# Two parts a row with borders that return every 16 steps, in all four sweeps of a recurrent convolution

## The chip, the cores and the metric

The kernel runs on one core of a Trainium2 chip. A core has five engines that run side by side: TensorE (PE, with its weight loads PEld) multiplies matrices, VectorE (DVE) and ScalarE (ACT) work element by element, GpSimd (POOL) does too and more slowly, and SyncE (SP) issues transfers. Each takes its instructions from a queue of its own and waits at semaphores for the others. Matmul results land in PSUM[...]; everything else lies in SBUF[...]. The metric is the device time of one execution in microseconds, lower is better.

## The reference

Four layers work on an image of 48 channels and 128 x 128 pixels in fp32, each added to its input: an attention over all pixels, sweeps, a patch convolution with an FFT, and a state-space scan. The change is in the second layer. `step` there is a recurrence: the next row is the input row plus a convolution of the row just computed, with five taps along the row and 48 x 48 channels.

```python
def step(w, b):
    def f(carry, inp):
        nxt = inp + _conv1d(carry, w, b)
        return (nxt, nxt)
    return f
xs = jnp.moveaxis(x, 2, 0)
d0 = xs[0]
_, d_rest = jax.lax.scan(step(down_w, down_b), d0, xs[1:])
D = jnp.concatenate([d0[None], d_rest], 0)
seq = jnp.concatenate([D[Hh - 3::-1], D[Hh - 1:Hh]], 0)
u0 = D[Hh - 1]
_, u_rest = jax.lax.scan(step(down_w, down_b), u0, seq)
...
_, r_rest = jax.lax.scan(step(right_w, right_b), r0, ws[1:])
...
_, l_rest = jax.lax.scan(step(left_w, left_b), l0, R[Ww - 2::-1])
```

So there are four sweeps of 127 steps each: down and up over rows, right and left over columns, and each step needs the whole of the step before it.

## The kernel before

`attention`, `sweeps`, `patch_conv` and `scan` are called one after the other. `sweeps` gets two large SBUF tiles: `other` (xb in the profile), whose view `t` holds the image by rows with three padding rows and columns, and `xq` (xa), whose view `u` holds it by columns. Partitions 0 to 47 and 64 to 111 hold the same channels one pixel apart, so that one matmul covers two taps, and three matmuls (`i` in 0, 1, 2) cover the five taps and the bias. ScalarE normalises the input into `t` in chunks of rows (34 instructions at line 699), while the down sweep already runs behind it. In the up sweep ScalarE copies finished rows into `u` (`turn`, line 735). After the up sweep's rows are free, SP loads x1 back into `other` (line 784), and in the left sweep GpSimd adds the finished columns to it (line 788), and VectorE takes statistics of the sum (`stretch`, line 750).

The recurrence is a chain: matmuls of a step, VectorE's addition (line 769), matmuls of the next step. To keep TensorE busy while VectorE adds, a row of 129 places is cut into parts, and the parts are issued in turn: `advance(n, m, lo, hi)` (line 755) issues for part m of step n six matmuls into `sums_of[m][n % 2]`, each a PSUM bank, and one addition. An fp32 matmul shows in the profile as two matmul records with a weight load each, so a part has twelve. A place needs two neighbours to either side of the step before, so the border between two parts moves two places to the left with every step: a part then needs nothing of the part to its right. `parts` (line 728) writes these borders: `cuts` start to the right of their middle place, end to the left of it, and jump back after `length` steps. At the jump the left part has to wait for the right part of the step before.

`plan` (line 771) uses three parts and 12 steps for down, up and right, and two parts and 16 steps for left. `act`, `pe` and `dve` are wrapped in `InOrder`, which keeps each engine's instructions of this stage in the order in which they are written. Instructions of other stages may be put between them by the scheduler. One such is of interest: `packed_weights` of `patch_conv` loads two weight tables on ScalarE's queue (lines 109 and 111) and multiplies them on VectorE (line 112), and line 825 adds a bias. Their places in VectorE's queue lie within the down sweep.

```python
cuts = [L * m // streams + size - 1 - 2 * at for m in range(1, streams)]
yield first + k, list(zip([0, *cuts], [*cuts, L]))
```

Of the kernel before, what the change touches and what calls it, by code (L numbers as in the profile page):

```python
# [19 lines left out]
F32 = mybir.dt.float32  # L20
# [9 lines left out]
CH = 512  # L30
# [620 lines left out]
def sweeps(ctx, tc, xq, other, x1, const, ins):  # L651
# [10 lines left out]
    ps = ctx.enter_context(tc.tile_pool(name="l1_ps", bufs=1, space=PSUM))  # L662
# [27 lines left out]
    keep_running(nc.tensor, idle, const["ident"], some, 2)  # L690
    off = pool.tile([C, 1], F32, name="off")
    nc.vector.scalar_tensor_tensor(off, mean, -1.0, rstd, ALU.mult, ALU.mult)
    sums_of = [[ps.tile([128, CH], F32, name=f"p{m}{k}") for k in range(2)] for m in range(3)]
    for p in sums_of[0] + sums_of[1] + sums_of[2]:
        nc.vector.memset(p[0:K, 0:L], 0.0)
    act = InOrder(tc, nc.scalar)
    for lo, hi in [(0, 2), (2, 8)] + [(r, r + 8) for r in range(8, H, 8)]:
# [19 lines left out]
    steps = []  # L717
# [8 lines left out]
    down, up, right = H - 1, 2 * (H - 1), 3 * (H - 1)  # L726

    def parts(first, count, streams, length):

        for k in range(count):  # L730
            at, size = k % length, min(length, count - k // length * length)
            cuts = [L * m // streams + size - 1 - 2 * at for m in range(1, streams)]
            yield first + k, list(zip([0, *cuts], [*cuts, L]))

    def turn(h):

        for at, y in ((0, E + h), (64, E + h - 1)):
            act.copy(
                u[at : at + C, :, y : y + 2].rearrange("c w y -> c y w"),
                t[0:C, E + h : E + h + 2, E : E + W],  # L740
            )
# [8 lines left out]
    def stretch():  # L750
        _, xr = todo.pop(0)
        dve.bn_stats(const["st2"][:, len(done), :], xr)
        done.append(xr)

    def advance(n, m, lo, hi):

        which, out, inp, state = steps[n]
        p = sums_of[m][n % 2]
        for i in range(3):
            for at, a, b in ((0, max(lo, 1), hi), (64, lo, min(hi, L - 1))):  # L760
                pe.matmul(
                    p[at : at + C, a:b],
                    lhsT=w[0:K, which, i, at : at + C],
                    rhs=state[0:K, 2 * i + a : 2 * i + b],
                    start=(i == 0),
                    stop=(i == 2),
                )
        here = slice(E - 1 + lo, E - 1 + hi)
        dve.tensor_add(out[0:K, here], p[0:K, lo:hi], inp[0:K, here])

    plan = [
        *parts(0, up, 3, 12),
        *parts(up, right - up, 3, 12),
        *parts(right, len(steps) - right, 2, 16),
    ]
    for n, streams in plan:
        for m, (lo, hi) in enumerate(streams):
            advance(n, m, lo, hi)
        if down <= n < up and (n - down) % 2 == 0:
            turn(H - 2 - (n - down))  # L780
        if n + 1 == up:

            for r in range(0, N, 2048):
                nc.sync.dma_start(other[0:C, r : r + 2048], x1[:, r : r + 2048])
        x = 4 * (H - 1) - 1 - n
        if n >= right and x in sums:
            xr = sums[x]
            nc.gpsimd.tensor_add(  # L788
                xr,
                xr,  # L790
                u[0:C, x : x + xr.shape[2], E : E + H].rearrange("c w h -> c h w"),
            )
            step = CH // 2 // xr.shape[2]
            todo += [(n + 8, xr[:, r : r + step]) for r in range(0, H, step)]
        if todo and n >= todo[0][0]:
            stretch()
# [823 lines left out]
def tile_kernel(ctx: ExitStack, tc: tile.TileContext, ins: dict, out: bass.AP):  # L1620
# [10 lines left out]
    with ExitStack() as image:  # L1631
        xp = image.enter_context(tc.tile_pool(name="image", bufs=1))


        const["l1_w"] = xp.tile([128, 3, 3, 64 + C], F32, name="l1_w")
        xa = xp.tile([128, W * (W + 6)], F32, name="xa")
        xb = xp.tile([128, (H + 6) * (W + 6)], F32, name="xb")
        for i in range(0, N // 2, 2048):
            nc.gpsimd.memset(xb[32:64, i : i + 2048], 0.0)
            for half in range(2):  # L1640
                at = half * N // 2 + i
                nc.sync.dma_start(
                    xb[64 * half : 64 * half + C, i : i + 2048], ins["x"][:, at : at + 2048]
                )
        nc.sync.dma_start(const["l1_w"], ins["l1_w"])
        attention(tc, xa, xb, x1, const, ins)
        sweeps(tc, xa, xb, x1, const, ins)
        patch_conv(tc, xb, xa, x3, const, ins)
        scan_stats(tc, const)
# [198 lines left out]
```

## Time and profile before

| what | us |
|---|---|
| runs | 7446.85, 7449.31, 7458.15; median 7449.31 |
| the profiled execution, its own time | 7442.33 |
| its span, first to last instruction | 7440.4 |
| attention, about | 0 to 3785 |
| sweeps: first to last addition | 3786.99 to 4309.82 |
| patch convolution and start of the scan | from 4310 |
| first scan instruction of VectorE | 4780.5 |
| last scan instruction of VectorE starts | 7417.4 |

The profile is of one execution. Engine names are as above; a group or timeline line gives start and length in us, the engine, the source line, the operation, the tiles written and read, the shape, how many instructions are merged, and in brackets the idle time of the engine before it and what released it. L48 is the line of the `InOrder` helper, so all wrapped instructions carry it, and tiles tell them apart: `p<-xb,l_w` is a matmul of the down or up sweep, `p<-xa,l_w` one of the right or left sweep. Starts and lengths are of this execution only, and ends of matmuls are modelled. The costliest groups of the sweeps on the page are these:

| group of the page | count | busy us | mean ns |
|---|---|---|---|
| matmul p<-xb,l_w (down, up) | 9144 | 227.6 | 213 |
| matmul p<-xa,l_w (right, left) | 7620 | 229.3 | 218 |
| addition xb<-p,xb | 762 | 154.0 | 203 |

Matmuls overlap, so the mean length of one is not the distance between two.

### The profile page before, as it was taken

Reading aid. Unit: us, or ns where it says so; the run is one execution under the profiler, and the core shown is the slowest. Engines: PE = TensorE matmul, PEld = TensorE weight load, DVE = VectorE, ACT = ScalarE, POOL = GpSimd, SP = SyncE. Lnnn points to the kernel's source line nnn. Section 1 sums busy time; section 2 is a strip of 40 time slices with the busy share of each in tenths; the row PEclk is TensorE's granted clock in tenths of the full one; section 3 lists DMA queues with packets and bytes.
Section 4 is the critical chain, followed back from the end, with each engine's and each line's share of the span. In section 5 each row is a group of like instructions: output and inputs, shape, how many; then the busy total and the mean of one; then the engine's idle time right before and its main releaser. Section 6 shows DMA issues by size and latency. Waiting matters only on the chain.

```text
span 7440.4 us, 230057 instructions
## 1 busy us (share of the span) xinstructions
PE 6069.1 (82%) x106542; PEld 3125.0 (42%) x106542; DVE 3510.9 (47%) x3414; ACT 4386.6 (59%) x4744; POOL 2803.7 (38%) x603
## 2 busy tenths in 40 slices
PE   8999999999999999999988999555545645554565
PEld 3333333333333333333367865244434434344444
DVE  7300000000000000000045544599999999999998
ACT  2566666666666666666634013466666666666665
POOL 1000000000000000000010122499999999999998
PEclk9999999999999999999999999776766767766666
DMA  3000000000000000000000010365566666656675
GB/s 66 8 4 4 4 3 4 4 3 4 4 3 4 4 3 4 4 4 3 4 12 21 4 48 19 89 166 153 165 159 165 158 159 158 162 157 165 180 181 146
DMA packets 182477, 486.35 MB, mean 65 GB/s; under 512 B 35972, under 2 KB 67763, under 8 KB 179603
## 3 DMA queue, kind: packets, MB, share of 16 engines
q1 hardware_dynamic: 174679, 464.21, 24.3%
q8 instruction: 835, 13.68, 0.8%
q10 hardware_dynamic: 6827, 7.35, 0.4%
q14 instruction: 136, 1.11, 0.1%
HBM read 427.91 MB, written 22.02 MB: 60 GB/s over the span
## 4 chain that ended last, share of the span: by engine, by line
PE 62%; DVE 23%; issue 7%; POOL 4%; ACT 2%; DMA 1%; SPq 0%; ACTq 0%; DVEq 0%; POOLq 0%
PE acc L48 24%; PE s L48 24%; DVE h L1595 21%; PE p L48 7%; POOL h L1588 3%; PE y L48 3%; PE pv L48 1%; PE pp L48 1%; PE pc L48 1%; PE po L48 1%; ACT dA L48 1%; DMA du<-rep 1%; DVE y L48 0%; POOL y L991 0%; POOL y L992 0%
## 5 line engine op out<-in xcount | busy, mean ns | idle before, releaser
L48 ACT ACTIVATE e<-s,absT 128x1024 f32<-128x1024 f32 x2048 | 2276.8, 1114 | 1197.6 <-PE s L48 1196.7
L1588 POOL TENSOR_TENSOR h<-du,bt 128x3072 f32<-128x3072 f32 (+1 forms) x386 | 2559.5, 6668 | 86.3 <-DMA du<-rep 61.0
L48 PE MATMUL s<-xa,xb 49*64 49x512 f32 x16384 | 2124.2, 588 | 1.3 <-POOL xb L320 1.3
L48 PE MATMUL acc<-e,xb 64*64 64x512 f32 x16384 | 2124.2, 588 | 1.0 <-ACT e L48 1.0
L1595 DVE TENSOR_TENSOR_SCAN h<-dA,carry,h 128x1024 f32<-128x1024 f32 x864 | 1939.9, 2324 | 42.6 <-ACT dA L48 27.4
L48 ACT ACTIVATE dA<-dt,a 128x1024 f32<-128x1024 f32 x1152 | 1287.3, 1118 | 871.2 <-DVE h L1595 860.2
L48 PE MATMUL y<-h,cw 128*32 128x48 f32 x49152 | 905.0, 247 | 926.9 <-issue 495.6
L421 DVE TENSOR_TENSOR both<-o 128x512 f32<-128x512 f32 x31 | 21.5, 692 | 2958.5 <-ACT o L48 2854.8
L681 POOL MEMSET xb<- 32x2064 f32 x8 | 14.6, 1819 | 3500.4 <-PE acc L48 3491.3
L48 PEld LDWEIGHTS y<-h,cw 128*32 128x32 f32 x49152 | 815.0, 141 | 1054.2 <-issue 650.9
L48 PEld LDWEIGHTS s<-xa,xb 49*64 49x64 f32 x16384 | 629.7, 132 | 1132.4 <-issue 581.8
L48 PEld LDWEIGHTS acc<-e,xb 64*64 64x64 f32 x16384 | 629.3, 132 | 1133.1 <-issue 1109.9
L1595 DVE TENSOR_TENSOR_SCAN h<-dA,h 128x1024 f32<-128x1024 f32 x288 | 635.6, 2270 | 42.9 <-ACT dA L48 35.0
L48 PE MATMUL yz<-ev,sel 128*8 128x48 f32 x4096 | 193.2, 260 | 275.5 <-ACT ev L48 264.3
L48 PEld LDWEIGHTS yz<-ev,sel 128*8 128x8 f32 x4096 | 162.5, 106 | 332.2 <-ACT ev L48 297.0
L48 PE MATMUL p<-xb,l_w 112*48 112x43 f32 (+20 forms) x9144 | 227.6, 213 | 41.6 <-issue 32.0
L48 PE MATMUL p<-xa,l_w 112*48 112x43 f32 (+30 forms) x7620 | 229.3, 218 | 25.9 <-issue 18.2
L48 PEld LDWEIGHTS p<-xb,l_w 112*48 112x48 f32 x9144 | 216.8, 125 | 53.2 <-issue 42.0
L48 PEld LDWEIGHTS p<-xa,l_w 112*48 112x48 f32 x7620 | 207.0, 125 | 48.1 <-DVE xa L48 23.0
L48 DVE TENSOR_TENSOR xb<-p,xb 112x54 f32<-112x54 f32 (+3 forms) x762 | 154.0, 203 | 111.9 <-PE p L48 65.6
L788 POOL TENSOR_TENSOR xb<-xb,xa 48x2048 f32<-48x2048 f32 (+2 forms) x10 | 45.0, 4502 | 422.0 <-DVE xa L48 398.8
L48 PE MATMUL pc<-wt,xa 128*128 128x288 f32 x768 | 198.1, 415 | 0.0
(204 smaller groups left out, 3148.2 us busy)
## 6 DMA issues: line engine op xcount, KB each, us to landing
du<-rep SPq DMA_DIRECT2D x768, 256.0 KB
dt<-rep SPq DMA_DIRECT2D x768, 256.0 KB
rep<-dd SPq DMA_DIRECT2D x24, 192.0 KB
yd<-ys ACTq DMA_DIRECT2D x256, 12.0 KB
rest<-xa SPq DMA_DIRECT2D x90, 38.0 KB
xb<-in_x_dram SPq DMA_DIRECT2D x8, 384.0 KB
xres<-in_x_dram SPq DMA_DIRECT2D x32, 96.0 KB
x<-xa SPq DMA_DIRECT2D x32, 96.0 KB
```

What stands on the lines that cost most here:

```text
L48: ins = method(*args, **kwargs).ins
L421: nc.vector.tensor_add(self.both, o[:, 0], o[:, 1])
L681: nc.gpsimd.memset(b[32:64, some, inside], 1.0)
L788: nc.gpsimd.tensor_add(xr, xr, u[0:C, x : x + xr.shape[2], E : E + H].rearrange("c w h -> c h w"),)
L1588: nc.gpsimd.tensor_mul(h[:, p, ks], du.unsqueeze(1).to_broadcast([128, ks.stop - ks.start, LC]), r["bt"][:, ks],)
L1595: nc.vector.tensor_tensor_scan(h[:, p, k, :], dA, h[:, p, k, :], carry[:, i, k : k + 1] if ci else 0.0, ALU.mult, ALU.add,)
```

## The change

The first three sweeps get the cut of the fourth: two parts, borders that return every 16 steps. As `parts` now runs over two sweeps at a time (down and up, right and left, 254 steps each), the groups of 16 continue across the turn. The third pair of PSUM banks and its two memsets go.

```diff
-    sums_of = [[ps.tile([128, CH], F32, name=f"p{m}{k}") for k in range(2)] for m in range(3)]
-    for p in sums_of[0] + sums_of[1] + sums_of[2]:
+    sums_of = [[ps.tile([128, CH], F32, name=f"p{m}{k}") for k in range(2)] for m in range(2)]
+    for p in sums_of[0] + sums_of[1]:
         nc.vector.memset(p[0:K, 0:L], 0.0)
...
-    plan = [
-        *parts(0, up, 3, 12),
-        *parts(up, right - up, 3, 12),
-        *parts(right, len(steps) - right, 2, 16),
-    ]
-    for n, streams in plan:
+    for n, streams in [*parts(0, up, 2, 16), *parts(up, len(steps) - up, 2, 16)]:
         for m, (lo, hi) in enumerate(streams):
             advance(n, m, lo, hi)
```

In the built programs the instructions of attention, patch convolution and scan stand in the same order before and after. In the sweeps, VectorE's queue has 131 additions ahead of the weights' product (line 112) before the change and 93 after it; lines below the edit carry numbers smaller by five after it (825 becomes 820).

## The prediction

> **What bounds the kernel now.** I read the page's chain of waits first, then the table of windows for the four sweeps, then the timelines of TensorE and VectorE inside them. The chain says that the end of the program is reached through TensorE for most of the span:
>
> ```profile
> PE 62%; DVE 23%; issue 7%; POOL 4%; ACT 2%; DMA 1%; SPq 0%; ACTq 0%; DVEq 0%; POOLq 0%
> ```
>
> Attention, sweeps, patch convolution and scan follow each other, so time saved inside the sweeps stays saved unless their first or last wait changes. The windows, one line a sweep (down, up, right, left; columns: busy time of PE, PEld, DVE, ACT, POOL with counts, granted clock, DMA share, GB/s):
>
> ```profile
> 3786.00:3920.00 134.00, 114.61 (x4582) 109.70 (x4582) 78.29 (x382) 39.64 (x33) 16.31 (x18) 0.99 0.06 16
> 3920.00:4055.00 135.00, 113.02 (x4572) 107.10 (x4567) 77.31 (x382) 83.27 (x127) 0.00 (x0) 1.00 0.11 25
> 4057.00:4190.00 133.00, 114.42 (x4557) 109.17 (x4553) 77.27 (x380) 0.00 (x0) 0.00 (x0) 0.98 0.03 7
> 4190.00:4310.00 120.00, 113.94 (x3048) 96.86 (x3048) 71.76 (x312) 0.00 (x0) 58.19 (x27) 1.00 0.01 3
> ```
>
> Each sweep has 127 steps of 129 columns. The left one, already in two parts, is 13 to 15 us shorter than the others although VectorE also does statistics in it and GpSimd additions. It has 3048 matmul records (127 x 2 parts x 6 x 2 passes) against 4572. The same line of code thus runs in both forms in this one trace. TensorE's timeline says why, first a piece of the right sweep, then of the left:
>
> ```profile
> 4103.13 3.08 PE L48 MATMUL p<-xa,l_w 112*48 112x42 f32 x128 [0.67 <-issue]
> 4107.15 3.37 PE L48 MATMUL p<-xa,l_w 112*48 112x49 f32 x128 [0.94 <-issue]
> 4110.90 3.08 PE L48 MATMUL p<-xa,l_w 112*48 112x52 f32 x128 [0.38 <-issue]
> ...
> 4205.31 14.73 PE L48 MATMUL p<-xa,l_w 112*48 112x78 f32 x384 [0.35 <-DVE xa L48]
> ```
>
> With three parts TensorE stops for 0.4 to 0.9 us after every 128 matmuls, and nothing that the profile shows released it ("issue"). With two parts 384 run without a stop, and only the restart of the borders (16 steps) makes a wait for VectorE. 128 matmuls with their 128 weight loads are 256 instructions, and the instruction queue q8 moves 13.68 MB in 835 packets, 16.4 KB each: one packet is one such run.
>
> [...] here a block lasts 3.08 us and the next begins 3.75 us after the one before (4107.15 to 4110.90). [...] after the pause before 3834.31 the window 3834.10:3837.50 has clock 0.51. [...]
>
> **The change part by part.**
>
> *1. The step.* Three sweeps lose a third of their matmuls, weight loads and additions: 381 steps x 1 part, so 381 x 12 = 4572 matmul records and 381 additions of about 0.2 us. The columns stay 129. The price of a two-part step is read from the restarts (the 79-column additions) of the left sweep on VectorE's timeline:
>
> ```profile
> 4205.97 0.48 DVE L48 TENSOR_TENSOR xa<-p,xa 112x79 f32<-112x79 f32 x2 [0.72 <-PE p L48]
> ...
> 4221.05 0.48 DVE L48 TENSOR_TENSOR xa<-p,xa 112x79 f32<-112x79 f32 x2 [0.72 <-PE p L48]
> ```
>
> 15.08 us for 16 steps, restart included: 0.9425 us a step, 39 ns a matmul, so a block of 128 lasts 5.03 us and the 3.75 us refill fits, with 1.28 us to spare. Now the present spans. Down and up, from first to last addition: 3786.99 to 4054.61, 267.6 us. Right and left: 4057.00 to 4309.82, 252.8 us. After, each pair is one run of 254 steps: 254 x 0.9425 = 239.4, less some 0.4 because the last group is short and ends without the wait for its successor: 239.0. Gain 28.6 + 13.8 = 42.4 us.
>
> *2. What the gain must give back.* VectorE's queue holds, between the sweeps' additions, the product of the next stage's weights (L112). In the built program it stands behind 131 additions before (43 2/3 steps) and behind 93 after (46 1/2 steps): later in steps, earlier in time. Its inputs do not move: their DMAs are issued by ScalarE, behind its 34 normalisations, whose waits name none of the sweep's additions.
>
> ```profile
> 3785.01 41.27 ACT L48 ACTIVATE xb<-xa,off,gn_rstd 48x256 f32<-48x256 f32 x34 [0.47 <-DVE off L692]
> ...
> 3826.31 0.36 ACTq L109 DMA_DIRECT2D w<-in_l_w_dram  x1
> ...
> 3834.01 1.36 DVE L112 TENSOR_TENSOR wt<-wt,w 128x1152 f32<-128x1152 f32 x1 [2.22 <-DMA beta<-in_l_beta_dram]
> ...
> 3834.31 1.94 PE L48 MATMUL p<-xb,l_w 112*48 112x46 f32 x39 [2.58 <-issue]
> ```
>
> So the data is there at 3834.0 in both. After, the 93rd addition ends near 3787.0 + 43.3 = 3830.3 (two groups of 15.08 and fourteen faster steps of about 0.91, plus its own 0.24). VectorE then waits 3.7 us, multiplies for 1.36, and two additions later does L825 for 0.45; behind it stand the next addition and therefore TensorE. 5.5 us, less about 0.3 for the addition that is ready meanwhile: 5.2. (The before spans contain their own such hole, so nothing is subtracted twice.) TensorE is idle for over 3 us, so one window of 3.4 us at half clock follows: there 96 matmuls of 43 columns took 3.4 us (4062.80:4066.20, clock 0.51), 35 ns each; for 64 columns I estimate 53 ns against 39, 0.9 to 1.0 us lost. I take 1.0 (bounds 0 and 2).
>
> *3. The turn from up to right.* VectorE's pause of 2.39 us before 4057.00 lies between my two spans and remains: it is two copies of ScalarE of 0.65 us and what follows. The half-clock window behind it remains too, 1.0. The fetch stall of 1.92 us before 4062.21, beside the last reload of x1 (0.79 MB), is inside the present span; with 1.28 us to spare I leave 0.5 of it (0 to 1.9).
>
> *4. The rest.* At the start, step 1 still waits for its row (0.68 us before 3788.36): 0.3. The two memsets of PSUM that go are free, TensorE's warm-up matmuls end later than they do. ScalarE's turning copies, 128 x 0.658 = 84 us, still fit under an up sweep of 120 us. GpSimd's additions in the left sweep keep their place in steps; the eight reloads that they read are issued on SP during the up sweep, the last at 4055.97, and the first addition comes at 4204.4, still over 130 us later. No other instruction of any queue is moved, and the work behind the sweeps is the same.
>
> Given back: 5.2 + 1.0 + 1.0 + 0.5 + 0.3 = 8.0. **Net 34.4 us.** The profiled execution took 7442.33 (span 7440.4), so 7407.9 on its own terms. It lay 7.0 below the median of the runs, 7449.31; the difference is what carries over, so the forecast is 7449.3 - 34.4 = **7415 us**.
>
> **The rivals.**
> *A, the holes cost nothing:* the whole 42.4, 7407. For it: the left rate includes work on VectorE that the others lack. Against: the wait at the weights follows from two times that don't move. 12 in 100.
> *B, the fetch binds again:* eight reloads of 384 KB run in the up sweep beside the refills. If each cost the 1.92 us seen at 4062.21, 15.4 us go and 7430 is left. Against: in the present up sweep, with no slack at all, the loss against the down sweep is about 1 us in all (135 against 134 us). 8 in 100.
> *C, slower: the clock.* The new sweeps issue a third fewer matmuls[...]. At 53 ns a matmul a step takes 24 x 53 = 1.27 us, 0.33 more; from 34.4 / 0.33 = 104 of the 381 steps on it decides against the change, and over all of them it gives 7415 + 126 = 7541. Against: the left sweep had clock 1.00 over 120 us with TensorE 95% busy. 5 in 100.
> That the change does not do what it says is excluded: the built program has 79 to 49 columns a part from the first step on.
>
> **How the numbers follow.** The forecast has 75 in 100. Its own range: the step rate to 0.01 us over 381 steps is 4 us, the holes 3, and the runs before differ by 11 among themselves, so a median may be off by 5; together 7404 to 7428, which also takes in A and part of B, and leaves C and the rest of B out. A measurement of this kernel can tell about 0.2%, 15 us, from no change. Faster by more: 75 + 12 + 5 of B = 92; within: 3 of B; slower: C, 5.
>
> **What would show it.** Right: runs of TensorE of 384 matmuls from the down sweep on, no "issue" stops of 0.4 to 0.9 us there; additions of 79 columns every 15.1 us; each of the four sweeps near 120 us, the down one near 126; a pause of VectorE before L112 of 3 to 4 us with its end at an unmoved 48 us after the first normalisation. Wrong: clock near 0.5 in the first three windows, "issue" stops in the up sweep, or L112 released later than that.

## The result, and the profile after

| | kernel before | changed kernel |
|---|---|---|
| runs | 7441.78 to 7458.15, median 7448.68 (5 runs) | 7408.55 to 7415.31, median 7409.21 (5 runs) |
| profiled execution, its own time | 7442.33 | 7415.31 |
| span of that execution | 7440.4 | 7413.5 |

The ratio after to before is 0.9949, with a 95% interval of 0.9934 to 0.9963: 28 to 49 us faster, the medians 39.5 apart. The forecast was 7415, 34.4 us below 7449.3, the median of the three runs known then; the measured median lies inside its range of 7404 to 7428.

The profiled pair is only 26.9 us apart, so the stages have to be told apart before anything is explained. The additions of the sweeps, of the changed kernel, are these (count, then duration minimum/median/maximum in ns, then the start of the first and of the last one, then shapes):

```profile
L48 DVE TENSOR_TENSOR xb<-p,xb x508: 200/226/243, 3786.3 to 4031.1; 112x77 f32<-112x77 f32 x6, 112x54 f32<-112x54 f32 x6, 112x71 f32<-112x71 f32 x6, 112x60 f32<-112x60 f32 x6
L48 DVE TENSOR_TENSOR xa<-p,xa x508: 184/225/242, 4033.6 to 4273.0; 112x77 f32<-112x77 f32 x6, 112x54 f32<-112x54 f32 x6, 112x71 f32<-112x71 f32 x6, 112x60 f32<-112x60 f32 x6
```

With the last addition's own length the four sweeps run from 3786.25 to 4273.27. The same starts and ends, with the first scan instruction of VectorE and the span, cut each execution into four stages:

| profiled execution | first addition at | sweeps | to the first scan instruction | scan to the end |
|---|---|---|---|---|
| before | 3787.0 | 522.8 | 470.7 | 2659.9 |
| changed | 3786.3 | 487.0 | 469.1 | 2671.2 |
| changed, run again (e10, below) | 3786.1 | 487.7 | 471.0 | 2667.1 |

The sweeps are 35.8 us shorter, and 487 comes out twice. The 11 us that the profiled execution of the changed kernel lost are in the scan, whose instructions are the same and whose length differs by 10 us and more between executions (among all profiles of this study from 2652 to 2671; why, no run shows). That is why a pair of executions says little, and medians or the stage itself must be compared. The windows of the changed kernel, one line a sweep, with the columns of the prediction's table (the column before the last two is the granted clock):

```profile
3786.00:3911.00 125.00, 114.47 (x3052) 98.44 (x3047) 58.87 (x257) 38.79 (x32) 16.30 (x18) 0.97 0.05 16
3911.00:4031.50 120.50, 112.57 (x3036) 95.58 (x3036) 57.39 (x254) 83.15 (x127) 0.00 (x0) 1.00 0.12 26
4033.00:4154.00 121.00, 114.18 (x3068) 97.60 (x3066) 57.38 (x255) 0.00 (x0) 0.00 (x0) 0.99 0.03 7
4154.00:4273.50 119.50, 113.13 (x3036) 95.99 (x3030) 71.88 (x310) 0.00 (x0) 58.24 (x27) 1.00 0.01 3
```

All four now look like the old left sweep, with about 3050 matmul records instead of 4570 and the clock near 1; down alone is some 5 us longer. TensorE's timeline inside the right sweep, where it had stopped after every 128 records (a timeline line joins records of several shapes and names the first; inside it no gap is longer than 0.15 us):

```profile
4094.32 14.72 PE L48 MATMUL p<-xa,l_w 112*48 112x78 f32 x384 [0.35 <-DVE xa L48]
...
4109.38 14.73 PE L48 MATMUL p<-xa,l_w 112*48 112x78 f32 x384 [0.35 <-DVE xa L48]
```

384 records run without an "issue" stop, one border cycle of 15.06 us from line to line, as read from the old left sweep. Over all four sweeps, TensorE's "issue" stops (us in total, times, longest) were before:

```profile
PE p L48 <- issue: 50.2, 80, 2.6
```

and are after the change:

```profile
PE p L48 <- issue: 0.8, 2, 0.5
```

The instruction queue q8 has 799 packets in the whole kernel where it had 835: 36 fewer, and the 4572 records that went are 35.7 blocks of 128. And VectorE where the weights' product stands in its queue:

```profile
3829.25 0.48 DVE L48 TENSOR_TENSOR xb<-p,xb 112x76 f32<-112x76 f32 x2 [0.45 <-PE p L48]
3831.36 1.36 DVE L112 TENSOR_TENSOR wt<-wt,w 128x1152 f32<-128x1152 f32 x1 [1.63 <-DMA wt<-in_l_dw_dram]
3832.64 0.35 DVE L48 TENSOR_TENSOR xb<-p,xb 112x78 f32<-112x78 f32 x2
3832.90 0.45 DVE L820 TENSOR_TENSOR wt<-wt,bdw 128x288 f32<-128x288 f32 x1
3833.60 0.24 DVE L48 TENSOR_TENSOR xb<-p,xb 112x80 f32<-112x80 f32 x1 [0.25 <-PE p L48]
3835.06 0.24 DVE L48 TENSOR_TENSOR xb<-p,xb 112x79 f32<-112x79 f32 x1 [1.21 <-PE p L48]
```

The wait that was foretold is there, shorter (1.63 us). VectorE took its queue in order here, as the prediction assumed: the next addition, of 78 columns, starts at 3832.64, behind the product, though TensorE had ended its matmuls at 3830.4. After it the additions come more slowly for a while. The clock column of four windows explains this:

```profile
3830.00:3834.00 4.00, 1.05 (x32) 0.78 (x26) 2.23 (x5) 0.00 (x0) 0.00 (x0) 0.93 0.33 99
3834.00:3838.00 4.00, 4.00 (x72) 3.99 (x72) 1.14 (x5) 0.00 (x0) 0.00 (x0) 0.50 0.02 4
3838.00:3842.00 4.00, 3.98 (x95) 3.73 (x93) 1.57 (x7) 0.00 (x0) 0.00 (x0) 0.72 0.00 0
3842.00:3846.00 4.00, 3.91 (x114) 3.39 (x112) 2.03 (x9) 0.00 (x0) 0.00 (x0) 1.00 0.02 6
```

TensorE had 2.5 us with nothing to do, and then ran at half clock (0.50) for 6.8 us, from 3833.4 to 3840.2: 72 matmul records in 4 us instead of the 110 of such a window at clock 1.00 (3834 to 3838 in e3, below).

### The profile page after: what moved, and what is told of

Same layout as the page of the kernel before. It is cut to its first block, busy times and chain, and to the rows that moved or that the text cites. A ratio compares the mean times of both kernels' runs of the same rounds, so it can differ in the third digit from the quotient of the medians.

```text
span 7413.5 us, 220408 instructions
## 1 busy us (share of the span) xinstructions
PE 6051.7 (82%) x101970; PEld 3057.1 (41%) x101970; DVE 3451.0 (47%) x3031; ACT 4389.3 (59%) x4744; POOL 2804.1 (38%) x603
## 4 chain that ended last, share of the span: by engine, by line
PE 61%; DVE 22%; issue 7%; POOL 5%; ACT 2%; DMA 2%; SPq 0%; ACTq 0%; DVEq 0%; POOLq 0%
PE acc L48 24%; PE s L48 24%; DVE h L1590 20%; PE p L48 7%; POOL h L1583 4%; PE y L48 3%; DMA du<-rep 1%; PE pv L48 1%; PE pp L48 1%; PE pc L48 1%; PE po L48 1%; DVE xb L48 1%; ACT dA L48 1%; ACT xb L48 1%; DVE y L48 0%
## 5 line engine op out<-in xcount | busy, mean ns | idle before, releaser
L48 PE MATMUL p<-xb,l_w 112*48 112x78 f32 (+8 forms) x6096 | 227.5, 224 | 19.3 <-DVE xb L48 8.9
L48 PE MATMUL p<-xa,l_w 112*48 112x78 f32 (+8 forms) x6096 | 227.5, 224 | 14.4 <-DVE xa L48 5.5
L48 PEld LDWEIGHTS p<-xb,l_w 112*48 112x48 f32 x6096 | 194.5, 124 | 52.9 <-DVE xb L48 35.4
L48 DVE TENSOR_TENSOR xb<-p,xb 112x79 f32<-112x79 f32 (+7 forms) x508 | 114.6, 226 | 129.4 <-PE p L48 113.5
```

What stands on the lines that cost most here:

```text
L48: ins = method(*args, **kwargs).ins
```

## The experiments

The theory: the three-part sweeps were held by the supply of TensorE's instructions, 128 matmul records with their loads at a time, and two parts need a third fewer of them. The rivals: a cost that every record has on TensorE itself, the additions and the number of parts, or the less frequent return of the borders. The first two experiments put instructions back without columns, parts or additions.

**e1 and e2: more matmuls, the same columns.** The edit to the changed kernel, with `SPLIT = (2,)` in e1 and `(1, 2)` in e2, cuts the matmuls of one or two of the three pairs into two halves of their columns:

```diff
+                mid = [(a + b) // 2] if i in SPLIT else []
+                end = b
+                for a, b in zip([a, *mid], [*mid, b]):
-                pe.matmul(
+                    pe.matmul(
...
-                    stop=(i == 2),
+                        stop=(i == 2 and b == end),
```

> Two parts, 16 steps, but the last tap's two matmuls of every part are cut into two halves of their columns: 32 matmul records a step instead of 24, the same columns, additions and borders. Theory (blocks of 128 matmuls with their loads can't be had faster than every 3.75 us, 29.3 ns a matmul): 32 x 29.3 = 0.938 us, just within the 0.9425 us of a step, so no more than 10 us over the changed kernel, about 7410 to 7420. Rival (every matmul costs TensorE some 22.5 ns of its own, the pace of three parts between their stops): 8 x 22.5 = 0.18 us a step, 508 steps, +91: 7500. Rival (parts and their additions decide, not matmuls): 7409.

> As e1_split32, with the middle tap cut too: 40 records a step. Theory: 40 x 29.3 = 1.172 us a step, +0.23 x 508 = +117: 7526, with an issue stop after every 128 matmuls and the blocks of q8 3.75 us apart. Rival (22.5 ns a matmul): 16 x 22.5 = 0.36, +183: 7590, without such stops. Rival (parts and additions decide): 7409.

Measured: e1 7445.6 us, ratio to the kernel before 1.0001 (0.9992 to 1.0010); e2 7507.4, ratio 1.0085 (1.0067 to 1.0104). No expectation for e1 was met: the theory had 7410 to 7420, the rivals 7500 and 7409. TensorE's timelines, first e1:

```profile
4118.16 15.92 PE L49 MATMUL p<-xa,l_w 112*48 112x78 f32 x512 [0.33 <-DVE xa L49]
```

then e2:

```profile
4140.20 3.58 PE L49 MATMUL p<-xa,l_w 112*48 112x30 f32 x128 [0.51 <-issue]
4143.95 3.89 PE L49 MATMUL p<-xa,l_w 112*48 112x73 f32 x137 [0.16 <-issue]
4148.17 10.25 PE L49 MATMUL p<-xa,l_w 112*48 112x78 f32 x375 [0.33 <-DVE xa L49]
4158.65 3.58 PE L49 MATMUL p<-xa,l_w 112*48 112x30 f32 x128 [0.24 <-issue]
```

In e1 a whole cycle of 512 records runs without an "issue" stop, as the theory said; yet the cycle is 16.26 us (4118.16 to 4134.42, where the next one begins), 1.016 us a step instead of 0.9425. Four more records in a part cost 0.073 us, 18 ns each. They lie on the chain of that part: its next addition waits for them. That such a chain sets the step of two parts can be seen in the changed kernel, where VectorE waits for TensorE in step after step, and TensorE's weight loads, 24 a step, for VectorE:

```profile
3827.66 0.74 PEld L48 LDWEIGHTS p<-xb,l_w 112*48 112x48 f32 x24 [0.18 <-DVE xb L48]
3828.31 0.49 DVE L48 TENSOR_TENSOR xb<-p,xb 112x74 f32<-112x74 f32 x2 [0.42 <-PE p L48]
3828.59 0.74 PEld L48 LDWEIGHTS p<-xb,l_w 112*48 112x48 f32 x24 [0.19 <-DVE xb L48]
```

So a step of two parts is set by the chain (matmuls of one part, addition, and the ways between), which both the theory and the rivals had left out. That e1 ends at the time of the kernel before is chance: its sweeps have another limit. In e2 some of the stops are back (46 in the sweeps, 20.6 us in all, where the theory had one after each of 159 blocks), and the cycle of 640 records, five blocks, takes 18.5 us (4140.20 to 4158.65), 3.69 us a block. That is the pace of the three-part sweeps (3.75) with other parts and other columns, and 1.15 us a step was near the theory's 1.17. But two thirds of the way from 0.9425 are again the longer chain (about 1.09 at 18 ns a record), and 375 records run without a stop, so e2 supports the theory and doesn't settle it.

**e5 and e8: the supply by itself.** Ahead of the sweeps, 3 x 512 matmuls (1024 records of each of three widths) that wait for nothing are added to the changed kernel. In e5 all write the same 48 partitions:

```diff
+    for wide in (8, 40, 80):
+        taps = w[0:K, 0, 0, 0:C]
+        keep_running(nc.tensor, idle[0:C, 0:wide], taps, const["ident"][0:K, 0:wide], 512)
```

> The changed kernel with 3 x 512 fp32 matmuls ahead of the sweeps that wait for nothing, have 48 columns of weights and stream 8, 40 and 80 columns (1024 records of each kind, 8 blocks of 128), and six more warm-up matmuls. Only the time of the added stretch is read. Theory (fetch): with 8 and with 40 columns the same pace, a block of 128 every 3.5 to 3.75 us and stops that nothing releases, 28 to 30 us for each kind; with 80 columns a pace of its own, slower than that and without stops. Rival (a matmul's own cost): the 8-column stretch is clearly faster than the 40-column one, 128 in under 3.2 us, with no stops. Whole time about 7409 + 100.

It came out at 7651.8 us, over 240 us more than the changed kernel instead of 100, and the added stretch answered another question. The windows of e5, roughly the parts with 8, 40 and 80 columns (the third begins with some 17 us of 40 columns):

```profile
3782.00:3852.00 70.00, 70.00 (x910) 70.00 (x908) 0.00 (x0) 0.00 (x0) 0.00 (x0) 0.52 0.01 2
3852.00:3925.00 73.00, 73.00 (x915) 73.00 (x915) 0.00 (x0) 0.00 (x0) 0.00 (x0) 0.50 0.01 2
3925.00:4014.00 89.00, 89.00 (x1235) 89.00 (x1234) 0.00 (x0) 0.00 (x0) 0.00 (x0) 0.88 0.01 2
```

It takes some 80 ns a record for both 8 and 40 columns (70 / 910 and 73 / 915), at half clock though TensorE was never idle. A block of 128 then lasts 10 us, so the supply of instructions is never asked for more, and neither the foretold blocks of 3.5 to 3.75 us nor the stops came. It failed as a test. In e8 the matmuls alternate between the two groups of output partitions, as those of a part do:

```diff
+    for wide in (43, 64, 24):
+        for k in range(256):
+            for at in (0, 64):
+                nc.tensor.matmul(
+                    idle[at : at + C, 0:wide],
+                    lhsT=w[0:K, 0, 0, at : at + C],
+                    rhs=const["ident"][0:K, 0:wide],
+                    start=True,
+                    stop=True,
+                )
```

> e5_fetch_alone mended: the added matmuls now alternate between the two groups of output partitions, 0 to 47 and 64 to 111, as those of a part do[...]. 512 fp32 matmuls (1024 records) each of 43, 64 and 24 columns. Only the added stretch is read. Theory (fetch): 43 columns run at 24 ns a record until the block ends and stop there, 3.5 to 3.8 us a block of 128, though these matmuls wait for nothing; 64 columns pace themselves at 33 to 35 ns, 4.2 to 4.5 us a block, without stops; 24 columns are no faster a block than 43, unless the clock falls. Rival (the stops of the three-part sweeps come from the chain of additions): 43 columns in 3.1 us a block without stops.

TensorE's timeline in the added stretch of e8 (whole time 7503.7 us):

```profile
3789.43 3.08 PE L692 MATMUL idle<-ident,l_w 112*48 112x43 f32 x128 [0.57 <-issue]
3793.45 3.08 PE L692 MATMUL idle<-ident,l_w 112*48 112x43 f32 x128 [0.94 <-issue]
3797.20 3.08 PE L692 MATMUL idle<-ident,l_w 112*48 112x43 f32 x128 [0.67 <-issue]
...
3811.63 31.52 PE L692 MATMUL idle<-ident,l_w 112*48 112x64 f32 x1152 [0.36 <-issue]
3843.41 3.06 PE L692 MATMUL idle<-ident,l_w 112*48 112x24 f32 x128 [0.27 <-issue]
3846.89 3.06 PE L692 MATMUL idle<-ident,l_w 112*48 112x24 f32 x128 [0.41 <-issue]
```

This settles it. Matmuls of 43 columns that wait for nothing show the very lines of the three-part sweeps: 128 records in 3.08 us, then a stop of 0.4 to 0.9. 24 columns make a block no quicker (3.06) and leave the same stops. A line's length includes some 0.2 us in which its last matmul ends, so the records begin 22.5 ns apart for both widths ((3.08 - 0.22) / 127), and a block comes every 3.5 to 4.0 us. It is not these matmuls themselves that need the stops: the first 311 records of the stretch ran without one, in 7.21 us. What ends the stops stands among the transfers of the same trace: one 16 KB packet of q8 comes for each block, and all 14 stops end 1.2 to 1.6 us after one has landed. In the kernel before, all 79 "issue" stops of the first three sweeps end 1.2 to 1.6 us after the landing of such a packet as well.

With 64 columns the stops are gone after the first of these blocks, though the pace was missed. The line of 1152 records joins two widths; the shapes apart, from 3811.5 to 3843.2, are:

```profile
L692 PE MATMUL idle<-ident,l_w 112*48 112x64 f32 x969 | 27.4, 219 | 0.4 <-issue 0.4
L692 PE MATMUL idle<-ident,l_w 112*48 112x24 f32 x183 | 4.3, 203 | 0.0
```

So 64 columns take 28 ns a record (27.4 us for 969), not 33 to 35. From this TensorE's own work in a step of two parts is, as an estimate, 24 x 28 = 0.67 us of 0.9425; the rest is TensorE waiting on the chain.

**e6: three parts, borders every 16 steps.** One edit to the kernel before: `3, 12` becomes `3, 16` in the first two lines of `plan`.

> The kernel before, with its three parts but borders that return every 16 steps in the first three sweeps: 36 records a step as before, a quarter fewer returns. Theory (fetch of 36 records sets the step): no change from the kernel before, within 5 us of it. Rival (fewer returns made part of the gain): 4 to 15 us faster than the kernel before.

7444.9 us, ratio to the kernel before 1.0005 (0.9996 to 1.0013). TensorE's timeline in its right sweep:

```profile
4103.05 3.10 PE L48 MATMUL p<-xa,l_w 112*48 112x38 f32 x128 [0.40 <-issue]
4106.52 3.45 PE L48 MATMUL p<-xa,l_w 112*48 112x53 f32 x128 [0.37 <-issue]
4110.26 3.11 PE L48 MATMUL p<-xa,l_w 112*48 112x56 f32 x128 [0.29 <-issue]
```

The stops are still there, and a rarer return of the borders alone gains nothing.

**e9: three parts, two thirds of the matmuls.** In the kernel before, `for i in range(2)` in place of `range(3)` (and `stop=(i == 1)`): the third pair of matmuls, with the last one or two of the five taps, is left out, and the output is another.

> The kernel before with the third matmul pair of every part left out (the last one or two of the five taps), so its output is another: three parts and three additions a step as before, but 24 records instead of 36. Only the first three sweeps are read, 401 us before. Theory (fetch at 29.3 ns a record): 0.70 us a step, about 268 us, with stops. Rival (TensorE's own pace of 24 ns): 0.58, about 220. Rival (parts and their additions, 0.27 us each, set the step): 0.81 or more, 310 and over.

The additions of down and up run from 3786.5 to 3977.5, 191 us against 267.6 before, 0.75 us a step (7315.0 us in all). The rival of parts and additions needed over 206 us and falls: with the same parts and additions the sweeps can go faster than they did. For the supply e9 shows nothing: 0.75 lies above both the theory's 0.70 and the 0.58 that was expected of TensorE by itself, and the foretold stops are not in the timeline:

```profile
3856.89 24.29 PE L48 MATMUL p<-xb,l_w 112*48 112x53 f32 x816 [0.15 <-DVE xb L48]
```

It takes 29.8 ns a record. VectorE is busy for 80% of the down sweep there (89.9 of 113 us), so the chain of a part is the likelier limit; no run separates it.

**e3, e4, e7: what is left to gain.** e3 moves the weights' product behind step 56 by an order without a wait; e4 sets both lengths to 12; e7 has both.

```diff
+        if n == 56:
+            const["behind"] = dve.last
...
-    nc.vector.tensor_mul(wt, wt, w1)
+    ins = nc.vector.tensor_mul(wt, wt, w1).ins
+    if behind is not None:
+        tc.add_manual_dep(
+            ins,
+            behind.name,
...
```

> The changed kernel, with the weights' product placed behind the additions of step 56 on VectorE, past the landing of its loads. Theory: VectorE's wait of about 3.5 us goes, the product's 1.8 us stays, and the half-clock window behind the wait goes: the down sweep is 4 to 5.5 us shorter, 7404. Rival (the product was covered by slack of the sweep): no change, 7409.

> Two parts, borders that return every 12 steps. Theory: a return costs 0.5 us (2.40 us for the last two steps of a group in place of 1.9) and there are 43 of them instead of 32, +5.5; the parts stay more alike, about 0.0125 us less a step, -6.4: together -1, 7404 to 7412. Rival (the longer cycle of 16 was a good part of the gain): each return dearer, +15 and more, over 7424.

> Both small changes together: two parts, borders every 12 steps, and the weights' product behind the additions of step 56. Theory: the sweeps, first to last addition, are 4.7 (e3) + 1 to 2.5 (e4, both pairs) shorter than in the changed kernel, 480 to 482 us against 487.0; whole time 7402 to 7408, which the spread of a run may hide. Rival (no sum, since the half-clock windows only move): 485 us and more.

| | time, median | ratio to before | sweeps in the profile |
|---|---|---|---|
| changed | 7409.2 | 0.9949 (0.9934 to 0.9963) | 487.0 |
| e3, product late | 7408.5 | 0.9952 (0.9939 to 0.9966) | 482.3 |
| e4, length 12 | 7409.6 | 0.9949 (0.9935 to 0.9963) | 485.5 |
| e7, both | 7407.5 | 0.9955 (0.9941 to 0.9969) | 481.0 |

Each ratio is to the kernel before as it ran beside that kernel. The sweeps of all three are shorter, by 4.7, 1.5 and 6.0 us. e4 and e7 are near what the theory said; e3 only in sum, since it had 4 to 5.5 us for the down sweep alone, and that one is 3.3 shorter (from its first to its last addition 121.4 us, 124.7 in the changed kernel). In e3 the product no longer waits, and the clock of the windows from 3826 to 3842 is 1.00 throughout. Its line on VectorE's timeline, and one of these windows:

```profile
3838.83 1.36 DVE L112 TENSOR_TENSOR wt<-wt,w 128x1152 f32<-128x1152 f32 x1
```

```profile
3834.00:3838.00 4.00, 3.87 (x110) 3.24 (x108) 2.06 (x10) 0.00 (x0) 0.00 (x0) 1.00 0.01 4
```

The half-clock window behind the turn from up to right is missing in e3 too (clock 1.00 from 4028.4 to 4040), and its right sweep is 1.0 us shorter (119.1 after 120.1). The edit moves nothing there, so this is not a gain of the moved product. In the whole time these few us drown in the 10 us and more by which the scan differs. So e7 and the changed kernel ran once more, in turns.

**e10 and e11: the best version beside the changed one.**

> The changed kernel once more, on the same chip and in turns with e11_late_12_again, so that the two can be compared. Its sweeps, first to last addition, should again take 487 us, its time about 39 us less than the kernel before.

> The kernel of e7_late_12 beside e10_changed_again. If the 6 us that its sweeps are shorter reach the end, its median lies 4 to 8 us below that of e10; if the stages behind take them back, within 2 us.

e10: 7403.90 to 7413.68, median 7413.0, ratio to before 0.9947 (0.9934 to 0.9961). e11: 7396.61 to 7411.72, median 7403.9, ratio 0.9942 (0.9929 to 0.9956); sweeps 480.3 us. The medians are 9 us apart, in the direction of the 7.4 us in the sweeps and a little beyond the expected 4 to 8; the intervals overlap. The sweeps are shorter in both pairs of profiles; that the whole is shorter is likely and not shown.

## Why the prediction was right

*The step.* The 0.9425 us read from the old left sweep held in three sweeps: cycles of 15.06 us in the right sweep, and much the same in up and left. In down the cycle is 15.23 us (VectorE's additions of 79 columns at 3851.82, 3867.05 and 3882.28), over the whole sweep some 1.2 us that the sum didn't have; what lengthens it no run shows. Down and up were put at 245.5 us (239.0 + 5.2 + 1.0 + 0.3) and took 245.1; right and left at 240.5 (239.0 + 1.0 + 0.5) and took 239.7. The sum was 34.4, the sweeps gave 35.8. That down and up fit so closely is in part luck, as the next points show.

*The reason for it.* Shown by e8, with e6 and e9 against the other rivals: the supply of instruction blocks held the three-part sweeps. Not seen by the prediction: what holds the two-part step. It compared the 5.03 us of a block with the refill and found room, which is right, but the 39 ns a record are not TensorE's pace (28 by e8). They contain the wait for the chain, and e1 shows that a step grows by 18 ns for each record more in a part, before the supply is short.

*The hole at the weights.* The right place and the wrong size. The wait was put at 3.7 us and was 1.63, because the release was taken as fixed and wasn't: the product started at 3831.36 and not at 3834.01. Of these 2.7 us, 0.9 are that the whole stage began earlier in this execution (ScalarE's first normalisation at 3784.14 after 3785.01); from there to the product it took 47.2 us, and 49.0 before the change (the prediction wrote 48). The other 1.8 us are a shorter time from the issue of the tables' loads to the product. The additions ahead of the product were earlier too, by 0.6 us, which leaves 2.1 for the wait. From the issue at line 111 to the product it was 5.5 and 5.6 us in two executions of the changed kernel and 6.3 in e4, against 7.3 before the change and 6.7 in e6, both with three parts. That TensorE's smaller demand for instructions made room is thus possible; no run separates it. The half clock behind the wait was put at the 3.4 us that followed TensorE's pause of 2.58 us before the change (clock 0.51) and lasted 6.8 (clock 0.50). What the hole cost in all follows from e3: its down sweep is 3.3 us shorter, and the product still holds up the additions there by 1.0 us (16.23 us between the additions of 79 columns at 3830.83 and 3847.06, in place of 15.23). That is 4.3 us, where 5.2 + 1.0 = 6.2 had been charged. The 1.9 us too many made up for the slower cycles of down (1.2) and for two stops in the up sweep (0.7), which the sum didn't have.

*The turn from up to right.* The pause was foretold unchanged at 2.39 and is 2.23 us (VectorE before 4033.57). One half-clock window of 3.4 us follows (clock 0.50 from 4034.8 to 4038.2), as charged, and e3, whose right sweep has none and is 1.0 us shorter, confirms its price. The fetch stall beside the last reload did not return.

*The rivals.* A (no holes, 7407) lies near the measured median, but the holes are in the trace, so that is the scan's spread and not its mechanism. B (the supply binds again in the up sweep), one of the signs of being wrong, is there in small: two cycles of up have an "issue" stop, 0.38 us before 3983.78 and 0.47 before 4014.35, and take some 0.3 to 0.4 us longer than the others. C (half clock in the new sweeps) was the author's guess, and is refuted by 0.97 to 1.00 in the four windows.

## What to carry to other kernels

When an engine stops at equal distances for no reason that the profile shows, count the instructions between the stops: short matmuls can use up instructions faster than they arrive (here 128 records in 3.08 us, where a block came every 3.5 to 4.0 us), and then fewer and wider ones can win although the engine has gaps already (here 35.8 us of 522.8). If the same loop runs in two forms in one trace, its other form is the best price of a change. Look also at what another stage has queued between a chain's instructions: a product that waits for its data in the middle of the sweep cost the wait (1.63 us), and a stretch at half clock on top (6.8 us).

## What the runs showed of the hardware

A block of 128 fp32 matmul records with their weight loads (one 16 KB packet of the instruction queue) comes every 3.5 to 4.0 us when 43 or 24 columns use it up faster (e8). Such records then begin 22.5 ns apart, those of 64 columns 28 ns apart, with the matmuls in turn in two groups of output partitions (e8). With all of them in one group and 8 columns it was about 45 ns at full clock, in the first 3.5 us of e5 (77 records in 3.40 us), and 80 ns at half clock; why, no run shows. Matmuls that keep TensorE busy without a gap can still run at half clock: in e5, with 8 and 40 columns in one group of output partitions, the clock was 0.50 to 0.52 for 143 us.

A pause of TensorE of about 2.5 us was followed by half clock, but not always for the same time: for 3.4 us before the change (2.58 us of pause; clock 0.51 from 3834.10 to 3837.50) and for 6.8 us after it (2.51 us; 0.50 from 3833.4 to 3840.2). A pause of 1.77 us at the turn was followed by 3.4 us at half clock in the changed kernel (0.60 on average from 4034 to 4038) and one of 1.76 us by none in e3 (1.00). So what a pause cost varied between executions.

GpSimd was slower than VectorE at work element by element: in the profile before, its additions of 2048 columns took 5.59 us (2.7 ns a column), VectorE's product of 1152 columns 1.36 us (1.2 ns a column).
